# Second-level weight factors made by GpSimd instead of VectorE, with another order of some sums and reads

## The chip, the core and the metric

The kernel runs on one core of a Trainium2 chip. A core has five engines that work through their own instruction streams and wait for one another by semaphores: TensorE (PE in the profile; its weight loads are listed as PEld) multiplies matrices into PSUM banks, VectorE (DVE) and ScalarE (ACT) work on SBUF and PSUM, GpSimd (POOL) works on SBUF, and SyncE (SP) issues DMAs. The metric is the device time of one execution in microseconds; lower is better.

## The reference

64 batches of 256 tokens with 512 features, a 256 x 256 adjacency matrix of zeros and ones, four 512 x 512 weights and a bias. Two layers:

```python
h = relu(layernorm(x))
q, k, v = h @ Wq.T, h @ Wk.T, h @ Wv.T
rel = adj.T * (q @ k.T)
rel = rel / norm(rel, axis=2)
x = x + rel @ v
h = relu(layernorm(x))
x = x + (adj @ h) @ weight + bias
```

Everything is float32.

## The kernel before

The batches are worked on in 32 pairs. Since rel = h Wq.T Wk h.T, the kernel first makes one matrix M out of Wq and Wk (`m_sb`), and then, for each pair: g = h M (`project_g` or `g_by_two_levels`), v = h Wv.T (`project_v`, `v_by_two_levels`), the scores (`scores`), the update with v (`attend`, or `attend_and_v` in the steady state), the second norm (`ln1`), the product with the adjacency (`gather_steps`) and the product with `weight` (`mix_by_two_levels`).

The large products use Winograd's form of Strassen's scheme: each operand is cut in 2 x 2 blocks, and seven block products take the place of eight. Products 1, 2, 3 and 4 use blocks or one sum, 5, 6 and 7 use sums of blocks. The sums of the left operand are the four steps of `left_factors` (L166 to L178): step 0 makes the factor of product 7, step 1 (`total`) that of 5, step 2 that of 6, step 3 that of 3. The sums of the right operand are the four steps of `right_operands` (L128 to L140): step 0 makes the factor of 7, step 1 (`diff`) that of 5, step 2 that of 6, step 3 that of 4. Without a fourth room, `total` and `diff` are written over a block of the operand itself.

In a product, bank_a gathers products 1, 6, 7 and 4 one on top of the other, so each next product into it can start only when the sum so far has been read out, by a ScalarE copy for a first value and by a VectorE addition for later ones. bank_c gathers 5 and 3, and bank_b takes 2. `winograd_steps` gives the order; with `early` it is 1, 2, 5, 6, 3, 7, 4. `two_levels` (from pair 2 on) replaces products 2 and 3 by seven smaller products each, on 128 x 128 blocks. These small products are grouped as g1, g2, g3 and g4, and gathered in bank_e (`at_a`) and bank_d (`at_b`, `at_c`). Its parts a1, c5, a6, a7 and a4 are the first-level products, each followed by its read; `c` is a second read of bank_c for another block and has no product.

The second level needs sums of 128 x 128 blocks of the weights as well: `second_right` (L146) gives two sets of four `right_operands` steps for each of M (`m_second_steps`), Wv (`wv_second_steps`) and weight (`w_second_steps`), 24 instructions on VectorE. Step 1 of a set overwrites a block of the weight, which the first-level products 2 and 3 of pairs 0 and 1 still read.

The order of the work on TensorE, VectorE and ScalarE is the order in which the program is written: the code runs inside `manual_schedule(engines=in_order)`. `run_steps(steps, side)` issues each step of a product (its matmuls and its read) and then the instructions of `side` for that number, so that a side entry decides where in VectorE's and ScalarE's streams an instruction stands. GpSimd and SP take their work in the planner's order; GpSimd adds the bias to x (L723) and issues the output transfers (L794), SP the transfers that move 32 x 32 blocks for transposes (`place_blocks` L440, `place` L586) and most loads.

The stages that the change touches are `before_pairs` (M is made; VectorE's sums of Wq and Wk stand between the reads), `first_pairs` (pairs 0 to 3 started, the weights' second-level factors made), and `last_pairs` (the last three, a, b and c, where nothing follows that could fill the gaps). The transposition of a pair's h is eight VectorE instructions (`turned`, L450), after which the four sums of `new_ht` follow (`sums`, L173 to L176).

Of the kernel before, what the change touches and what calls it, by code (L numbers as in the profile page):

```python
# [9 lines left out]
F32 = mybir.dt.float32  # L10
# [3 lines left out]
ALU = mybir.AluOpType  # L14
# [5 lines left out]
def kernel(  # L20
# [38 lines left out]
    nc = tc.nc  # L59
    P = 128  # L60
    B, N, D = x.shape
    DC = D // P
    NC = N // P
# [5 lines left out]
    HT_ = T // 2  # L69
    HC = DC // 2  # L70
# [7 lines left out]
    work = ctx.enter_context(tc.tile_pool(name="work", bufs=1))  # L78
# [9 lines left out]
    def load(i, queue=nc.sync):  # L88
        X[i] = ring[i % len(ring)]
        queue.dma_start(out=X[i], in_=xs[i])  # L90
# [34 lines left out]

        return lambda j, k: w[:, j * HC : (j + 1) * HC, k * HD : (k + 1) * HD]

    def right_operands(b, t):  # L128

        sub = nc.vector.tensor_sub
        diff = t[3] if len(t) > 3 else b(0, 1)
        steps = [
            lambda: sub(t[1], b(1, 1), b(0, 1)),
            lambda: sub(diff, b(0, 1), b(0, 0)),
            lambda: sub(t[0], b(1, 1), diff),
            lambda: sub(t[2], b(1, 0), t[0]),
        ]
        return {1: b(0, 0), 2: b(1, 0), 3: b(1, 1), 4: t[2], 5: diff, 6: t[0], 7: t[1]}, steps  # L140
# [5 lines left out]
    def second_right(right, name):  # L146


        factors, steps = {}, []
        for n in (2, 3):  # L150
            t = const.tile([P, 3, P], F32, name=f"{name}_t{n}")
            factors[n], more = right_operands(
                lambda j, k, f=right[n]: f[:, j, ts(k, P)], [t[:, r] for r in range(3)]
            )
            steps += more
        return factors, steps

    def run(steps):
        for step in steps:
            step()  # L160

    def left_blocks(at):

        return lambda i, j: at[:, j * HC : (j + 1) * HC, i]

    def left_factors(a, s):  # L166

        v = nc.vector  # L170
        total = s[3] if len(s) > 3 else a(1, 0)
        steps = [
            lambda: v.tensor_sub(s[0], a(0, 0), a(1, 0)),  # L173
            lambda: v.tensor_add(total, a(1, 0), a(1, 1)),
            lambda: v.tensor_sub(s[1], total, a(0, 0)),
            lambda: v.tensor_sub(s[2], a(0, 1), s[1]),  # L176
        ]
# [642 lines left out]
    def before_pairs():  # L820
# [3 lines left out]
        pz = ps_m.tile([P, 512], F32, tag="pm", name="pz")  # L824
        for _ in range(8):
            nc.tensor.matmul(pz[:, :P], warm, warm, start=True, stop=True)
        m_left, left_steps = left_operands(
            work, wq_sb.rearrange("p c (h n) -> p c h n", h=NC), "ys", "m"
        )
        wk_t = work.tile([P, 4, HC, HD], F32, tag="hy", name="wk_t")  # L830
        m_factors, right_steps = right_operands(right_blocks(wk_sb), [wk_t[:, n] for n in range(4)])
# [1 line left out]
        stats, root, end, relus = ln0(0)  # L833
# [29 lines left out]
        def take(t, k, bank, first):  # L863
# [6 lines left out]

        look()
        transpose_adj()
        run([right_steps[1], left_steps[0], left_steps[1]])
        winograd(product_weights_moving(m_left, m_factors), take, {
            0: [load_wv],
            1: [left_steps[2], right_steps[2]],
            2: stats[0:2] + [lambda: load(1, nc.scalar)],
            3: [left_steps[3]] + stats[2:4] + [root, right_steps[0], lambda: load(2, nc.scalar)],
            4: [end] + relus + [right_steps[3]],
            5: m_steps[0:3] + [transpose_wv],  # L880
            6: m_steps[3:4],
# [48 lines left out]
    def first_pairs(exact):  # L930
# [26 lines left out]
            0: sums1[2:4] + masks[0:1], 1: masks[1:2] + squares[0:2] + stats[0:1],  # L957
            2: squares[2:4] + stats[1:2], 3: [norm_root] + stats[2:3],
            4: [inverse] + scales + [place] + stats[3:4] + [root], 5: [end] + w_steps[0:2],
            6: w_steps[2:4] + w_second_steps[0:4],  # L960
        })
        gs = g_operands(1)
        turned2, sums2 = transpose_blocks(2)
        project_v(1, {
            0: gs[0:2], 1: gs[2:3] + turned2[0:2], 2: gs[3:4] + turned2[2:4] + relus[0:2],
            3: turned2[4:6] + relus[2:4],
            4: turned2[6:8] + m_second_steps[0:4],
            5: m_second_steps[4:8] + turns[0:2], 6: turns[2:4],
        })
        place_blocks(3)  # L970
        masks, squares, norm_root, inverse, scales, place, turns = scores(1, {
            0: sums2[0:1], 1: sums2[1:2], 2: sums2[2:3], 3: sums2[3:4], 4: w_second_steps[4:8],
        })
        stats, *parts = ln1(0, exact)
        h_second = second_h.pop(2)()
# [4 lines left out]
        if exact:  # L980
            nc.vector.tensor_copy(adjt_r, adjt_sb)
        g, v = g_and_v(2, by_slot(layer_1(parts), {
            1: h_second + [inverse], 2: turned3[0:4], 3: scales + [place] + turned3[4:8],
            4: add_bias(0), 5: sums3[0:2],
        }))
        v_steps, rel_steps = attend_operands(1)
        y_products, y_steps = gather_steps(0, exact)
        run_steps(y_products, {
            0: wv_second_steps[0:4], 1: wv_second_steps[4:8], 2: y_steps[0:1], 3: v_steps[0:1],
        })  # L990
        y_second = second_of_y(0)
        totals, mean, row_squares, *norm0 = norm_by_scalar(flat(X[4]))
# [1 line left out]
        mixed = mix_and_v(0, g, v, {  # L994
            0: y_steps[2:4] + totals[0:2], 1: y_second[0:4] + totals[2:4],
            2: y_second[4:8] + [mean] + row_squares[0:2], 3: v_steps[1:2] + row_squares[2:4],
            4: turns + rel_steps[0:2] + norm0[0:2], 5: rel_steps[2:4] + v_steps[2:3] + sums3[2:4],
        })
        return norm0[2], v_steps[3:4], mixed, v

# [48 lines left out]
    def last_pairs(exact, relu0, v_last, mixed, v):  # L1049
# [37 lines left out]
        m = mix_by_two_levels(a)  # L1087
        root, end, relus, uppers, lowers = parts
        run_steps([
            m["a1"], m["c5"], lambda: run([m["a6"], m["c"]]), m["g1"], m["a7"], m["g2"], m["a4"],  # L1090
            m["g3"],
        ], {
            0: [root], 1: [inverse, end] + relus[0:2], 2: uppers[0:2],
            3: lowers[0:1] + relus[2:3], 4: lowers[1:2] + relus[3:4],
            5: uppers[2:4] + add_bias(b), 6: lowers[2:3], 7: lowers[3:4],
        })
        turn_at_once()
        m["g4"]()
# [8 lines left out]
        m = mix_by_two_levels(b)  # L1107
        root, end, relus, uppers, lowers = parts
        run_steps([
            m["a1"], m["c5"], lambda: run([m["a6"], m["c"]]), m["g1"], m["a7"], m["g2"], m["a4"],  # L1110
            m["g3"],
        ], {
            0: y_second[0:4] + [root], 1: y_second[4:8] + [end] + relus[0:2] + uppers[0:2],
            3: lowers[0:1] + relus[2:3], 4: lowers[1:2] + relus[3:4],
            5: uppers[2:4] + add_bias(c), 6: lowers[2:3], 7: lowers[3:4],
        })
        y_products, y_steps = gather_steps(c, exact)
        run_steps(y_products, {0: [m["g4"]], 2: y_steps[0:1]})
# [1 line left out]
        run(y_steps[1:2])  # L1120
        m = mix_by_two_levels(c)
        run_steps([
            m["a1"], m["c5"], m["g1"], lambda: run([m["a6"], m["c"]]), m["g2"], m["a7"], m["g3"],
            m["a4"], m["g4"],
        ], {0: y_steps[2:4] + y_second[0:4] + y_second[4:8]})

    first = dict(X), H[0]
    with tc.If(inexact < 1) as either:
# [33 lines left out]
```

## Time and profile before

| What | Value |
|---|---|
| median of 3 executions | 1709.56 us (1709.17 to 1711.31) |
| the profiled execution | 1708.38 us, its span 1706.3 us |
| TensorE busy | 1686.4 us (99%) |
| VectorE busy | 1479.2 us (87%) |
| ScalarE busy | 812.0 us (48%) |
| GpSimd busy | 213.0 us (12%) |
| first matmul starts, last one ends | 1.03 and 1700.14 us |

The span runs from the first to the last recorded instruction or transfer of the profiled execution; all times inside the kernel are counted from its start. In a timeline a row gives the start, the duration, the engine, the line, the operation, what it writes and reads, the shape, and how many instructions of that kind are merged in it. A bracket at the end gives how long the engine was idle before it, and what released it. In a row of TensorE, eight matmul records are one product of the first level.

### The profile page before, as it was taken

Reading aid. Unit: us, or ns where it says so; the run is one execution under the profiler, and the core shown is the slowest. Engines: PE = TensorE matmul, PEld = TensorE weight load, DVE = VectorE, ACT = ScalarE, POOL = GpSimd, SP = SyncE. Lnnn points to the kernel's source line nnn. Section 1 sums busy time; section 2 is a strip of 40 time slices with the busy share of each in tenths; the row PEclk is TensorE's granted clock in tenths of the full one; section 3 lists DMA queues with packets and bytes.
Section 4 is the critical chain, followed back from the end, with each engine's and each line's share of the span. In section 5 each row is a group of like instructions: output and inputs, shape, how many; then the busy total and the mean of one; then the engine's idle time right before and its main releaser. Section 6 shows DMA issues by size and latency. Waiting matters only on the chain.

```text
span 1706.3 us, 28450 instructions
## 1 busy us (share of the span) xinstructions
PE 1686.4 (99%) x10274; PEld 1530.5 (90%) x10274; DVE 1479.2 (87%) x3336; ACT 812.0 (48%) x1835; POOL 213.0 (12%) x167
## 2 busy tenths in 40 slices
PE   8999999999999999999999999999999999999998
PEld 7988999999999999999999999998999999999986
DVE  7888898888898888998888988888988889888777
ACT  4444545544445554445445455444455544453331
POOL 0011101111001111001111011110011110011111
PEclk9999999999999999999999999999999999999999
DMA  7414332234332343322343322433323433223101
GB/s 242 64 29 87 79 75 57 51 87 87 77 60 68 59 87 83 79 56 57 75 87 80 77 54 53 87 85 77 60 67 61 87 82 80 54 47 62 38 26 52
DMA packets 425734, 122.56 MB, mean 72 GB/s; under 512 B 398064, under 2 KB 398832, under 8 KB 425584
## 3 DMA queue, kind: packets, MB, share of 16 engines
q1 hardware_dynamic: 412992, 80.28, 25.5%
q0 software_dynamic: 8432, 32.51, 5.2%
q10 hardware_dynamic: 4160, 7.87, 1.3%
q8 instruction: 83, 1.36, 0.3%
q14 instruction: 67, 0.55, 0.1%
HBM read 38.27 MB, written 33.55 MB: 42 GB/s over the span
## 4 chain that ended last, share of the span: by engine, by line
PE 89%; DVE 5%; SPq 2%; ACT 1%; DMA 1%; issue 1%; DVEq 0%; ACTq 0%
PE bank_a L299 24%; PE bank_a L287 11%; PE bank_a L311 7%; PE bank_a L662 6%; PE bank_e L525 6%; PE bank_c L299 6%; PE py L739 6%; PE bank_d L525 5%; PE bank_c L311 3%; PE bank_c L287 3%; PE bank_c L662 3%; PE bank_e L478 3%; SPq L586 2%; PE bank_d L478 2%; PE bank_b L311 2%; PE bank_b L662 1%
## 5 line engine op out<-in xcount | busy, mean ns | idle before, releaser
L723 POOL TENSOR_TENSOR x_ring<-x_ring,bias_bc 128x512 f32<-128x512 f32 x128 | 188.2, 1491 | 745.1 <-DVE rel L559 437.1
L287 PE MATMUL bank_a<-ht,m_t 128*128 128x256 f32 x768 | 181.5, 379 | 0.6 <-DVE g L466 0.6
L299 PE MATMUL bank_a<-wv_t,ht 128*128 128x256 f32 x768 | 181.7, 379 | 0.0
L287 PEld LDWEIGHTS bank_a<-ht,m_t 128*128 128x128 f32 x768 | 145.8, 190 | 20.8 <-DVE g L466 1.0
L299 PEld LDWEIGHTS bank_a<-wv_t,ht 128*128 128x128 f32 x768 | 143.5, 190 | 18.3
L711 DVE TENSOR_TENSOR h<-h2c,h 128x512 fp32r<-128x512 f32 x128 | 86.5, 697 | 80.0 <-ACT h L707 80.0
L513 ACT COPY v<-bank_a 128x512 f32<-128x512 f32 x96 | 55.1, 574 | 207.9 <-PE bank_a L299 207.9
L364 ACT ACTIVATE blocks<-x_ring,sm 128x512 f32<-128x512 f32 x112 | 80.8, 722 | 125.1 <-DVE sm L361 123.3
L739 PE MATMUL py<-adjt_r,h 128*128 128x256 f32 x1024 | 126.8, 281 | 0.1
L342 ACT ACTIVATE h2c<-x_ring,nb,rs 128x512 f32<-128x512 f32 x128 | 97.5, 809 | 56.4 <-DVE nb L339 52.0
L299 PE MATMUL bank_a<-w_t,ys 128*128 128x256 f32 x512 | 121.4, 380 | 1.1 <-DVE x_ring L773 1.1
L739 PEld LDWEIGHTS py<-adjt_r,h 128*128 128x128 f32 x1024 | 120.8, 189 | 0.3 <-DVE h L711 0.3
L794 POOL DMA_DIRECT2D out_dram<-x_ring x31 | 24.0, 773 | 727.1 <-issue 525.8
L377 ACT ACTIVATE h<-x_ring,nb,rs 128x512 f32<-128x512 f32 x112 | 82.0, 802 | 65.9 <-PE bank_e L525 65.9
L299 PEld LDWEIGHTS bank_a<-w_t,ys 128*128 128x128 f32 x512 | 96.6, 190 | 15.1 <-DVE x_ring L773 1.9
L743 ACT COPY yt<-py 128x512 f32<-128x512 f32 x128 | 75.1, 587 | 71.5 <-PE py L739 44.7
L773 DVE TENSOR_TENSOR x_ring<-bank_a,x_ring 128x512 f32<-128x512 f32 x128 | 88.0, 687 | 22.4 <-PE bank_a L299 22.2
L311 PE MATMUL bank_a<-ht,gt 128*128 128x128 f32 x744 | 101.3, 279 | 0.4 <-DVE rel L559 0.4
L330 DVE BATCH_NORM_STATS2 st<-x_ring 128x6 f32<-128x512 f32 x144 | 97.9, 680 | 0.4
L557 ACT COPY rel<-bank_a 128x256 f32<-128x256 f32 x96 | 35.7, 372 | 130.4 <-PE bank_a L311 115.4
L311 PEld LDWEIGHTS bank_a<-ht,gt 128*128 128x128 f32 x744 | 90.4, 192 | 3.6 <-DVE rel L559 0.6
L450 DVE STREAM_TRANSPOSE ht<-blocks 128x256 f32<-128x256 f32 x248 | 87.6, 408 | 1.4 <-DMA blocks<-h 1.4
(221 smaller groups left out, 4006.4 us busy)
## 6 DMA issues: line engine op xcount, KB each, us to landing
blocks<-h SPq DMA_DIRECT2D x496, 64.0 KB, 2.3
out_dram<-x_ring POOLq DMA_DIRECT2D x31, 1024.0 KB, 4.8
x_ring<-in_x_dram SPq DMA_DIRECT2D x28, 1024.0 KB, 5.6
placed<-rel SPq DMA_DIRECT2D x496, 32.0 KB, 2.0
x_ring<-in_x_dram ACTq DMA_DIRECT2D x4, 1024.0 KB, 5.6
wq_sb<-in_L_gnn_Wq_dram SPq DMA_DIRECT2D x4, 256.0 KB, 5.0
wk_sb<-in_L_gnn_Wk_dram ACTq DMA_DIRECT2D x4, 256.0 KB, 6.0
wv_sb<-in_L_gnn_Wv_dram ACTq DMA_DIRECT2D x1, 1024.0 KB, 5.4
```

Source lines behind the costliest of these rows:

```text
L287: nc.tensor.matmul(bank[:, e * HT_ : (e + 1) * HT_], right[n][:, d, ts(e, P)], left[n][:, d, :], start=(start and e == 0 and d == 0), stop ...
L299: nc.tensor.matmul(bank[:, b * HD : (b + 1) * HD], left[n][:, d, ts(b, P)], right[n][:, d, :], start=(start and b == 0 and d == 0), stop=( ...
L311: nc.tensor.matmul(bank[:, ts(b, P)], right[n][:, d, ts(b, P)], left[n][:, d, ts(b, P)], start=(start and b == 0 and d == 0), stop=(d == H ...
L330: nc.vector.bn_stats(st[:, c, :], src[:, c, :])
L342: nc.scalar.activation(dst, src[:, c, :], AF.Relu, bias=nb[:, c : c + 1], scale=rs[:, c : c + 1])
L450: nc.vector.transpose(ht[:, d, half].rearrange("p (b n) -> p b n", b=NB), by_half[:, :, half, d])
L525: nc.tensor.matmul(out, left[k][n], right[k][n], start=start, stop=True, skip_group_check=True)
L662: nc.tensor.matmul(bank[:, ts(b, HD)], left[n][:, b], right[n][:, b], start=(start and b == 0), stop=True, skip_group_check=True,)
L711: nc.vector.tensor_sub(dst[:, 1, c, :], whole_h[c], dst[:, 0, c, :].bitcast(F32))
L723: (lambda c=c: add(xt[:, c, :], xt[:, c, :], bias_bc, ALU.add)) for c in range(TC)
L739: nc.tensor.matmul(pm[:, d, :], left[:, b * NC + m, ts(d0 + d, P)], right, start=(n == 0), stop=(n == len(terms) - 1),)
L773: nc.vector.tensor_add(xt[block], bank.rearrange("p (b e) -> p b e", b=NB), xt[block])
```

## The change

The 24 second-level steps of the weights are issued on GpSimd: `right_operands` gets the engine as a parameter, and `second_right` passes `nc.gpsimd`. They are no longer spread over the side entries but issued together: those of M and weight after `project_g(1)`, those of Wv after `place_blocks(3)`.

In `before_pairs`, Wq's `total` gets a room of its own (`m_room`), and the sums of Wq and Wk stand in another order among the reads and the statistics. In `first_pairs`, the sums of pair 2 and the transposes and sums of pair 3 stand at other side entries. In `last_pairs`, the second read of bank_c (`c`) follows product 7 instead of product 6, the differences `lowers` are issued two at a time and later, and the last pair's weight product takes its parts in the order of the other two, with the sums of y after its second product.

```diff
-    def right_operands(b, t):
-        sub = nc.vector.tensor_sub
+    def right_operands(b, t, engine=nc.vector):
         diff = t[3] if len(t) > 3 else b(0, 1)
+        def sub(out, x, y):
+            engine.tensor_tensor(out, x, y, ALU.subtract)
...
-                lambda j, k, f=right[n]: f[:, j, ts(k, P)], [t[:, r] for r in range(3)]
+                lambda j, k, f=right[n]: f[:, j, ts(k, P)], [t[:, r] for r in range(3)], nc.gpsimd
...
-        m_left, left_steps = left_operands(
-            work, wq_sb.rearrange("p c (h n) -> p c h n", h=NC), "ys", "m"
+        m_rooms = work.tile([P, 3, HC, HT_], F32, tag="ys", name="m_rooms")
+        m_room = work.tile([P, 4, 2, P], F32, tag="hs2", name="m_room")
+        m_room = m_room.rearrange("p a b n -> p (a b n)")[:, : HC * HT_]
+        m_left, left_steps = left_factors(
+            left_blocks(wq_sb.rearrange("p c (h n) -> p c h n", h=NC)),
+            [m_rooms[:, n] for n in range(3)] + [m_room.rearrange("p (c n) -> p c n", c=HC)],
...
-        run([right_steps[1], left_steps[0], left_steps[1]])
+        run([right_steps[1], left_steps[1]])
         winograd(product_weights_moving(m_left, m_factors), take, {
-            0: [load_wv],
-            1: [left_steps[2], right_steps[2]],
-            2: stats[0:2] + [lambda: load(1, nc.scalar)],
-            3: [left_steps[3]] + stats[2:4] + [root, right_steps[0], lambda: load(2, nc.scalar)],
+            0: [load_wv, left_steps[2], right_steps[2]],
+            1: [left_steps[3], left_steps[0]],
+            2: [right_steps[0]] + stats[0:1] + [lambda: load(1, nc.scalar)],
+            3: stats[1:4] + [root, lambda: load(2, nc.scalar)],
...
-            6: w_steps[2:4] + w_second_steps[0:4],
-        })
+            6: w_steps[2:4],
+        })
+        run(m_second_steps + w_second_steps)
...
-            4: turned2[6:8] + m_second_steps[0:4],
-            5: m_second_steps[4:8] + turns[0:2], 6: turns[2:4],
+            4: turned2[6:8], 5: turns[0:2], 6: turns[2:4] + sums2[0:1],
         })
         place_blocks(3)
+        run(wv_second_steps)
         masks, squares, norm_root, inverse, scales, place, turns = scores(1, {
-            0: sums2[0:1], 1: sums2[1:2], 2: sums2[2:3], 3: sums2[3:4], 4: w_second_steps[4:8],
+            0: sums2[1:2], 1: sums2[2:3], 2: sums2[3:4],
...
-            1: h_second + [inverse], 2: turned3[0:4], 3: scales + [place] + turned3[4:8],
-            4: add_bias(0), 5: sums3[0:2],
+            1: h_second + [inverse], 2: turned3[0:4], 3: scales + [place],
+            4: add_bias(0) + turned3[4:6], 5: turned3[6:8], 6: sums3[0:1],
...
-            0: wv_second_steps[0:4], 1: wv_second_steps[4:8], 2: y_steps[0:1], 3: v_steps[0:1],
+            0: sums3[1:3], 1: sums3[3:4], 2: y_steps[0:1], 3: v_steps[0:1],
...
-            4: turns + rel_steps[0:2] + norm0[0:2], 5: rel_steps[2:4] + v_steps[2:3] + sums3[2:4],
+            4: turns + rel_steps[0:2] + norm0[0:2], 5: rel_steps[2:4] + v_steps[2:3],
...
         run_steps([
-            m["a1"], m["c5"], lambda: run([m["a6"], m["c"]]), m["g1"], m["a7"], m["g2"], m["a4"],
+            m["a1"], m["c5"], m["a6"], m["g1"], lambda: run([m["a7"], m["c"]]), m["g2"], m["a4"],
             m["g3"],
         ], {
             0: [root], 1: [inverse, end] + relus[0:2], 2: uppers[0:2],
-            3: lowers[0:1] + relus[2:3], 4: lowers[1:2] + relus[3:4],
-            5: uppers[2:4] + add_bias(b), 6: lowers[2:3], 7: lowers[3:4],
+            4: lowers[0:2] + relus[2:4], 5: uppers[2:4] + add_bias(b), 7: lowers[2:4],
...
         run_steps([
-            m["a1"], m["c5"], m["g1"], lambda: run([m["a6"], m["c"]]), m["g2"], m["a7"], m["g3"],
-            m["a4"], m["g4"],
-        ], {0: y_steps[2:4] + y_second[0:4] + y_second[4:8]})
+            m["a1"], m["c5"], m["a6"], m["g1"], lambda: run([m["a7"], m["c"]]), m["g2"], m["a4"],
+            m["g3"], m["g4"],
+        ], {0: y_steps[2:4], 1: y_second})
```

The weight product of pair b changes as that of pair a does.

More of the change, by code (lines that the diff above doesn't have):

```diff
@@ L1109, in last_pairs @@
         run_steps([
-            m["a1"], m["c5"], lambda: run([m["a6"], m["c"]]), m["g1"], m["a7"], m["g2"], m["a4"],
+            m["a1"], m["c5"], m["a6"], m["g1"], lambda: run([m["a7"], m["c"]]), m["g2"], m["a4"],
             m["g3"],
@@ L1113, in last_pairs @@
             0: y_second[0:4] + [root], 1: y_second[4:8] + [end] + relus[0:2] + uppers[0:2],
-            3: lowers[0:1] + relus[2:3], 4: lowers[1:2] + relus[3:4],
-            5: uppers[2:4] + add_bias(c), 6: lowers[2:3], 7: lowers[3:4],
+            4: lowers[0:2] + relus[2:4], 5: uppers[2:4] + add_bias(c), 7: lowers[2:4],
         })
@@ L1122, in last_pairs @@
         run_steps([
-            m["a1"], m["c5"], m["g1"], lambda: run([m["a6"], m["c"]]), m["g2"], m["a7"], m["g3"],
-            m["a4"], m["g4"],
-        ], {0: y_steps[2:4] + y_second[0:4] + y_second[4:8]})
+            m["a1"], m["c5"], m["a6"], m["g1"], lambda: run([m["a7"], m["c"]]), m["g2"], m["a4"],
+            m["g3"], m["g4"],
+        ], {0: y_steps[2:4], 1: y_second})
     first = dict(X), H[0]
```

## The prediction

> **What bounds the kernel now.** I read the page's busy times first. TensorE (PE) works nearly all the time and VectorE (DVE) 87%; GpSimd (POOL) is almost idle.
>
> ```profile
> PE 1686.4 (99%) x10274; PEld 1530.5 (90%) x10274; DVE 1479.2 (87%) x3336; ACT 812.0 (48%) x1835; POOL 213.0 (12%) x167
> ```
>
> So only a wait of TensorE costs time. The waits, asked for the PE alone, name VectorE behind nearly all of them: results that VectorE reads out of a PSUM bank too late, or factors that it makes too late. The timeline puts them at the two ends of the run; between 140 and 1640 us the stalls are a few tenths each. Four places concern the change. First, the product of Wq and Wk:
>
> ```profile
> 13.48 0.69 DVE L137 TENSOR_TENSOR wk_t<-wk_sb,wk_t 128x512 f32<-128x512 f32 x1
> ...
> 14.31 1.97 PE L299 MATMUL bank_a<-wk_t,ys_m 128*128 128x256 f32 x8 [0.42 <-DVE wk_t L137]
> ...
> 16.50 1.97 PE L299 MATMUL bank_c<-wk_sb,ys_m 128*128 128x256 f32 x8 [0.22 <-DVE ys_m L176]
> ...
> 18.08 0.69 DVE L135 TENSOR_TENSOR wk_t<-wk_sb 128x512 f32<-128x512 f32 x1
> ```
>
> Three products in a row wait for a factor (the third, at 18.91, for the last row). A product of eight matmuls takes 1.73 us from start to start when nothing waits, so from the starts 12.00, 14.31, 16.50, 18.91 the true losses are 0.58, 0.46 and 0.68: 1.72 us. The brackets say less, because a matmul's end is modelled late. I use starts from here on.
>
> Second and third, in the first pairs, with the instructions that VectorE does ahead of the late read:
>
> ```profile
> 81.60 0.29 DVE L138 TENSOR_TENSOR m_t<-m_sb,m_t 128x128 f32<-128x128 f32 x1
> 82.00 1.43 DVE L589 STREAM_TRANSPOSE turned<-placed 128x256 f32<-128x256 f32 x4
> ...
> 86.77 1.16 PE L311 MATMUL bank_a<-ht,gt 128*128 128x128 f32 x8 [0.42 <-DVE rel L559]
> ...
> 103.64 2.72 DVE L450 STREAM_TRANSPOSE ht<-blocks 128x256 f32<-128x256 f32 x8
> ...
> 107.59 1.99 PE L287 MATMUL bank_a<-ht,m_t 128*128 128x256 f32 x8 [0.65 <-DVE g L466]
> ...
> 130.14 0.49 PE L525 MATMUL bank_e<-w_t,yt 128*128 128x128 f32 x2 [1.54 <-DVE x_ring L534]
> ...
> 132.00 0.69 DVE L175 TENSOR_TENSOR ht<-ht 128x512 f32<-128x512 f32 x1
> ...
> 132.71 0.69 DVE L176 TENSOR_TENSOR ht<-ht 128x512 f32<-128x512 f32 x1
> ...
> 134.06 1.13 PE L662 MATMUL bank_a<-placed,rel 128*128 128x256 f32 x4 [1.45 <-DVE x_ring L669]
> ```
>
> By starts these cost 0.59 (86.77), 0.80 (107.59), 1.70 (130.14) and 1.62 (134.06). Fourth, the last pairs' weight products, where the fourth product waits for the read of the one before:
>
> ```profile
> 1651.36 1.23 DVE L711 TENSOR_TENSOR h<-h2c,h 128x512 fp32r<-128x512 f32 x1
> ...
> 1653.25 1.99 PE L299 MATMUL bank_a<-w_t,yt 128*128 128x256 f32 x8 [0.45 <-DVE x_ring L773]
> ...
> 1678.49 1.17 DVE L711 TENSOR_TENSOR h<-h2c,h 128x512 fp32r<-128x512 f32 x1
> ```
>
> **What the Trainium skill says.** "SBUF — State Buffer", Who interferes with whom: a VectorE instruction with two SBUF inputs and a GpSimd instruction that reads SBUF lock each other out for a whole instruction. The trace agrees: the two L711 rows above took 1.23 and 1.17 us, each ending 0.55 us after a bias addition of GpSimd, and 0.68 elsewhere; a read that takes one input from PSUM kept its 0.69. "GPSIMD Engine Reference", Elementwise — side-by-side cycle accounting: a two-input add over 2048 elements takes 4497 ns. The trace has 1.28 us for 512 elements undisturbed (the first of the two at 1649.53). A line through both gives 2.1 ns an element and 0.2 us fixed: 0.47 us for 128 elements, an estimate. "Perfetto Trace Analysis", Tensor Engine Instruction: the end that the profile shows for a matmul is computed; hence starts.
>
> **Part 1, order of the Wq/Wk sums.** Same eight subtractions and additions; `total` gets a room of its own, so left_steps[1] need not follow left_steps[0]. VectorE's new order up to the product at 13.73 (12.00 + 1.73) is right 1, left 1, left 2, right 2. The last chunk of Wq lands at 8.88 and of Wk at 10.56, so right 2 ends about 11.3, ahead of bank_b's read at 12.27. Left 3 (12.88), left 0 (13.48), right 0 (14.08) follow at the 0.60 spacing of such rows, all before their products (15.46 and 17.19). TensorE could thus be 1.72 earlier. The four statistics now follow one another, and `root` stays at 18.00; without right 0 behind it, nb ends at 19.04 instead of 19.64. ScalarE then is the chain: relus 2.94, two copies of wvt, the copy of bank_a, four copies of ht, 6.5 us without the idle 0.83 it has today. The ht sum that the second product of project_g waits for ends at 26.28 and that product starts at 26.33 instead of 27.85. No moved step issues a DMA; the loads on ScalarE's queue keep their places behind the same copies, and SP's block transfers follow relus that come 1.5 earlier with the rest. Gain **1.5**.
>
> **Part 2, 24 second-level operations to GpSimd.** Each 128x128 row is 0.29 us on VectorE, 0.32 spaced: 7.8 us less there, of which 5.2 before 88 us. On GpSimd 24 x 0.47 = 11 us, where it does nothing before 99.12. The factors overwrite blocks that the whole first-level products read, so GpSimd starts m2 when TensorE has finished project_g(1)'s sixth product (67.2), w2 after w_steps, wv2 after project_v(1)'s sixth product (79.3): ready by about 71, 77 and 83, while the first user of m2 is at 99.8, of w2 at 119.3, of wv2 at 131.6. TensorE doesn't wait for them. POOL's queue holds only biases and output transfers behind them, the first at 99.12.
>
> The cost is the lock. Where w_steps and gs (eight two-input rows at 68.4 to 75.8) meet m2 and w2, the engines alternate. Each held row starts up to 0.47 later and runs 0.55: about 0.35 a row, six rows held, 2 us, against 1.3 us saved there (four w2 rows). bank_a's read in project_v(1) then ends about 0.4 later than its 78.28; TensorE needs it at 78.83, so nothing is lost. The unknown is the duration: 0.29 (the one-input GpSimd row on 128x128 at 1.20) to 1.28 (the 128x512 row). I take 0.47.
>
> After 80 us four m2 rows no longer fill the time in which the score blocks are in flight. The last of `placed` lands at 81.43, so the transposes start there, not at 82.00. To bank_a's read VectorE still does four transposes, four ht sums, two reads: 4.72 us as today, read done 86.22 against the 86.18 at which TensorE is free. Gain 0.59 - 0.09 = **0.5**.
>
> **Part 3, transposes and sums of pair 3.** Four of the eight transposes at 103.64 (1.33 us) leave the place ahead of bank_a's read, which ends 106.25 instead of 107.54, before TensorE is free at 106.79: 0.80 gained. They go behind lowers[2] and lowers[3]; with the sums moved into the gather in place of the eight wv2 rows, VectorE finishes yt's sum about 115.07 where TensorE, 0.8 earlier, wants it at 115.01: 0.1 back. Gain **0.7**. The stall at 130.14 stays: VectorE is idle 0.35 at 123.8, so it follows TensorE again, and its turns, rel sums and norm are as before. At 134.06 the two ht sums are gone: 2 starts 0.66 apart, 1.32 of the 1.62. Gain **1.3**.
>
> **Part 4, last pairs.** Pair a: the second read of bank_c and lowers[0] move behind the read of product 7, which ends 1652.58; the fourth product starts 1652.63, not 1653.25. But c and two lowers (0.6 each) now stand before g2's read, which ends 1654.71; g3 needs that bank at 1654.36 and starts 1654.76, not 1655.08. With the wait before g4 gone too, the gather starts 0.5 earlier; its fourth matmul of step 1 waits for lowers[3], which GpSimd's biases hold to about 1658.4: gain 0.45. Pair b: likewise g3 starts 1680.66 instead of 1680.46, and lowers[2:4], behind g3's reads and a bias that holds until 1683.15, end 1684.3 instead of 1684.12: loss 0.2. Pair c: all eight sums of y stand before a6's read, which ends 1694.0, so product 7 waits 1.3 us, in place of 1.56 us of stalls today; then g4 waits 0.45 for g3's read. The last read ends 1700.9 instead of 1700.75: loss 0.15. Together **+0.1**.
>
> Sum: 1.5 + 0.5 + 0.7 + 1.3 + 0.1 = 4.1 us. The profiled execution took 1708.38 (span 1706.3, 2.1 around it); it would be 1704.3. The median of three is 1709.56, 1.2 above the profiled one. I round to 4.0 for starts after waits: **1705.6**.
>
> **Rivals.** (1) VectorE held by GpSimd, ending slower. If a 128x128 GpSimd row takes as long as a 128x512 one (1.28), eight rows in project_v(1) come 8 x 1.2 - 1.3 - 0.55 = 7.7 us too late for bank_a's read, against 4.1 gained: 1713.2. It decides above (4.1 + 1.85)/8 + 0.1 = 0.84 us a row. For it: the 1.2 us L711 rows. Against: GpSimd's 128x128 row of 0.29. (2) The last pairs lose: lowers and y sums stand before reads at three places, and each may cost 0.7 more than I worked out if a bias falls badly: 1705.6 + 2 = 1707.6. For it: lowers already wait at 1678.49 today. (3) The prologue passes on only the 0.6 of nb (relus are then the chain), with half a microsecond held in part 2: 1707.0. (4) More: the stall at 130.14 shrinks, or the biases miss the lowers: 1704.3. (5) Nothing changes, the stalls being refilled by the next wait: 1709.5; against it, VectorE does 7.8 us less.
>
> **Numbers.** Main case 0.56 (1704.7 to 1706.5), rival 4 0.10, rivals 2 and 3 0.11 each, 5 0.05, 1 0.07. From 1704.0 to 1708.0 leaves out 5, 1 and the far edge of 4. About 0.2%, 3.4 us, is what a measurement tells from no change, so faster needs less than 1706.1: 0.47 of the main case, rival 4, and 0.14 of rivals 2 and 3, which lie around the edge; slower is rival 1; the rest is within.
>
> **What would show it.** No TensorE wait at 14 to 19, near 85 and 105 us; that of 130.14 still there at 1.5; that of 134.06 near 0.1; GpSimd rows of 128x128 near 0.47 from 65 to 83 us; new waits before g3 in the last pairs and before pair c's product 7. A GpSimd row over 0.8, or a wait before project_v(1)'s last product, proves me wrong; so does a start of the second project_g product later than 27.

## The result, and the profile after

| | before | changed | |
|---|---|---|---|
| median time | 1708.37 us (1707.29 to 1711.31, 17 runs) | 1705.60 us (1703.48 to 1707.79, 17 runs) | ratio 0.9981, 95% interval 0.9974 to 0.9989 |
| span of the profiled execution | 1706.26 us | 1701.41 us | 4.85 less |

The ratio says 3.2 us less, between 1.9 and 4.4; the medians differ by 2.8. The page's busy line after the change: TensorE's work is the same, VectorE has 24 instructions less, GpSimd 24 more.

```profile
PE 1684.2 (99%) x10274; PEld 1530.6 (90%) x10274; DVE 1472.9 (87%) x3312; ACT 811.3 (48%) x1835; POOL 226.7 (13%) x191
```

Line numbers from L138 to L826 are 3 higher than before, those further down 6 to 8, and the four steps of `right_operands` are now all L135. The timeline of the changed kernel, first at the product of Wq and Wk and the first two products of `project_g`:

```profile
13.71 1.89 PE L302 MATMUL bank_a<-wk_t,m_rooms 128*128 128x256 f32 x8
...
15.44 1.89 PE L302 MATMUL bank_c<-wk_sb,m_rooms 128*128 128x256 f32 x8
...
17.16 1.89 PE L302 MATMUL bank_a<-wk_t,m_rooms 128*128 128x256 f32 x8
...
23.52 1.93 POOL L135 TENSOR_TENSOR m_t<-m_sb 128x128 f32<-128x128 f32 x2 [22.02 <-ACT m_sb L874]
...
25.40 1.31 POOL L135 TENSOR_TENSOR wv_t<-wvt_sb 128x128 f32<-128x128 f32 x2
25.41 0.99 DVE L177 TENSOR_TENSOR ht<-ht 128x512 f32<-128x512 f32 x1 [0.28 <-ACT ht L434]
...
26.46 1.78 PE L290 MATMUL bank_c<-ht,m_sb 128*128 128x256 f32 x7 [0.44 <-DVE ht L177]
```

The three products stand 1.73 apart with no bracket: their waits are gone. The product at 26.46 is the one that started at 27.85. It still waits (0.60 by starts, 0.19 before): its sum L177 took 0.99 instead of 0.69, because GpSimd was reading beside it. These early GpSimd rows are steps 0 of M and Wv, which overwrite nothing, and which the planner put as early as their inputs allow. The rest of the second level, and what it does to VectorE:

```profile
65.97 0.46 POOL L135 TENSOR_TENSOR m_t<-m_sb 128x128 f32<-128x128 f32 x1
...
69.25 0.96 POOL L135 TENSOR_TENSOR w_sb<-w_sb 128x128 f32<-128x128 f32 x1 [2.29 <-DVE w_t L135]
...
69.81 0.94 DVE L135 TENSOR_TENSOR gt<-g 128x512 f32<-128x512 f32 x1
70.29 0.78 POOL L135 TENSOR_TENSOR w_t<-w_sb 128x128 f32<-128x128 f32 x1
...
79.80 1.42 DVE L592 STREAM_TRANSPOSE turned<-placed 128x256 f32<-128x256 f32 x4 [1.20 <-DMA placed<-rel]
```

A GpSimd row takes 0.45 to 0.46 when alone, and 0.78 to 0.96 where it meets the sums of g, which take 0.79 to 0.94 instead of 0.69. The score transposes now wait for their blocks to land, and no wait of TensorE is left at 85 us. Then the rest of the first pairs, and the last pairs:

```profile
104.70 1.89 PE L290 MATMUL bank_a<-ht,m_t 128*128 128x256 f32 x8
...
112.94 1.96 PE L302 MATMUL bank_c<-w_sb,yt 128*128 128x256 f32 x8
...
127.43 0.46 PE L528 MATMUL bank_e<-w_t,yt 128*128 128x128 f32 x2 [1.63 <-DVE x_ring L537]
...
129.93 1.13 PE L665 MATMUL bank_a<-placed,rel 128*128 128x256 f32 x4
...
1647.92 1.99 PE L302 MATMUL bank_a<-w_t,yt 128*128 128x256 f32 x8
...
1650.05 0.71 PE L528 MATMUL bank_e<-w_t,ys 128*128 128x128 f32 x4
...
1670.74 1.99 PE L302 MATMUL bank_a<-w_t,ys 128*128 128x256 f32 x8 [0.78 <-DVE x_ring L776]
...
1677.46 1.81 DVE L714 TENSOR_TENSOR h<-h2c,h 128x512 fp32r<-128x512 f32 x2
...
1689.20 1.99 PE L302 MATMUL bank_a<-w_t,ys 128*128 128x256 f32 x8 [1.14 <-DVE x_ring L776]
```

By starts the stalls are 0 (104.70), 0.25 (112.94), 1.79 (127.43), 0.22 (129.93), 0 (1647.92), 0.30 (1650.05), 0.94 (1670.74) and 1.30 (1689.20). What was 107.59, 130.14, 134.06 and 1653.25 is now 104.70, 127.43, 129.93 and 1647.92. The two differences of h at 1677.46 take 1.81 together; two of them take 1.28 where no bias addition runs.

For the experiments I cut every profiled execution at the same four instructions of TensorE and VectorE, counted from the span's start to its end. The first column ends at `project_g(0)`'s second product (27.85 before), the second at product 6 of the second attend (134.06), the third at the scores of pair b (1635.92), the fourth at VectorE's last read (1700.34), the last at the end of the span:

| us | start-up | first pairs | middle | last pairs | tail |
|---|---|---|---|---|---|
| before | 27.85 | 106.21 | 1501.86 | 64.42 | 5.92 |
| changed | 26.46 | 103.47 | 1501.21 | 64.70 | 5.57 |
| e_order | 26.79 | 106.53 | 1501.14 | 64.54 | 5.88 |
| e_gpsimd | 28.03 | 105.78 | 1503.08 | 64.43 | 5.94 |
| e_last | 27.78 | 106.53 | 1503.22 | 64.63 | 5.59 |
| e_vector | 26.65 | 107.94 | 1503.49 | 64.63 | 5.59 |
| e_pair3 | 28.06 | 105.76 | 1502.51 | 64.63 | 5.65 |
| e_long | 26.06 | 104.49 | 1503.99 | 64.61 | 5.60 |
| i_first | 26.58 | 101.93 | 1503.50 | 64.63 | 5.61 |
| i_last | 26.88 | 103.48 | 1501.96 | 64.35 | 5.60 |
| i_two | 26.57 | 101.95 | 1501.14 | 63.58 | 5.59 |
| i_three | 26.66 | 101.92 | 1503.60 | 62.76 | 5.61 |

The middle column is the same work in all twelve kernels (but for GpSimd's order in e_long and i_three), and differs by 2.9 us from one execution to another. The first column moves with the landing of Wq and Wk, and with TensorE's first microseconds: in e_pair3, for one, its matmuls are 0.43 apart instead of 0.22 until 12.85 us. So a single span can't tell these kernels apart. The columns of the first and the last pairs hold the places that the edits touch, but each comes from one execution, so I check them against the stalls.

### The profile page after: what moved, and what is told of

The parts are those of the page before. It is cut to its first block, busy times and chain, and to the rows that moved or that the text cites. A ratio compares the mean times of both kernels' runs of the same rounds, so it can differ in the third digit from the quotient of the medians.

```text
span 1701.4 us, 28459 instructions
## 1 busy us (share of the span) xinstructions
PE 1684.2 (99%) x10274; PEld 1530.6 (90%) x10274; DVE 1472.9 (87%) x3312; ACT 811.3 (48%) x1835; POOL 226.7 (13%) x191
## 4 chain that ended last, share of the span: by engine, by line
PE 91%; DVE 4%; SPq 2%; DMA 1%; ACT 1%; issue 1%; DVEq 0%; ACTq 0%
PE bank_a L302 24%; PE bank_a L290 12%; PE bank_a L314 7%; PE bank_c L302 6%; PE bank_e L528 6%; PE bank_a L665 6%; PE py L742 6%; PE bank_d L528 5%; PE bank_c L314 3%; PE bank_c L290 3%; PE bank_c L665 3%; PE bank_e L481 3%; SPq L589 2%; PE bank_d L481 2%; PE bank_b L314 2%; PE bank_b L665 1%
```

## Experiments: one part at a time

Each time below is a median beside runs of the kernel before on the same chip.

**Part 1 alone.** `before_pairs` as changed, all else as before (the diff is the one shown in the change).

> The kernel before with the new order of the sums of Wq and Wk alone (room of its own for total, sums ahead of the statistics). Theory: the three waits of TensorE between 14 and 19 us go, ScalarE then is the chain, and project_g's second product starts at 26.1 to 26.2 us: it started at 27.85 before and at 26.46 in the changed kernel, where one ht sum of VectorE took 0.99 instead of 0.69 beside GpSimd's first rows, which are not here. So 1.7 us less by the starts, and the stalls at 86.8, 107.6, 130.1 and 134.1 stay as before (0.6, 0.8, 1.7, 1.6). Rival: the gain of 1.7 needs nothing of the change but shows again as a longer stall behind it (scores or the first gather), and the whole is within 0.5 us of before.

Measured: 1708.43 us against 1709.89, ratio 0.9991 (0.9983 to 1.0000), which hardly tells it from before; the starts do:

```profile
11.21 1.56 PE L299 MATMUL bank_b<-wk_sb,wq_sb 128*128 128x256 f32 x6 [0.48 <-DMA wk_sb<-in_L_gnn_Wk_dram]
...
26.79 1.99 PE L287 MATMUL bank_c<-ht,m_sb 128*128 128x256 f32 x8
```

Counted from the product that waits for the last piece of Wk, so that the loads drop out, `project_g`'s second product comes 15.58 us later (26.79 - 11.21), against 17.25 before (27.85 - 10.60) and 15.88 in the changed kernel (26.46 - 10.58). The order gives 1.67, and GpSimd's early rows take 0.30 of it away again. The stalls behind stay (0.58, 0.80, 1.70, 1.62), and the first pairs are no shorter. They are in fact 0.3 longer: 0.34 is a stall in the scores of pair 0, where transposed blocks landed late; e_last, whose code there is that of before, has the same stall (its transposes start at 52.00, at 51.24 before). The rival falls: no stall that waits for a result of the sums refills the gain.

**Part 2 alone.** The engine changed, every side entry left where it was:

```diff
-                lambda j, k, f=right[n]: f[:, j, ts(k, P)], [t[:, r] for r in range(3)]
+                lambda j, k, f=right[n]: f[:, j, ts(k, P)], [t[:, r] for r in range(3)], nc.gpsimd
```

> The kernel before with the 24 second-level operations on GpSimd alone; every side entry otherwise as before. Theory: only the stall at scores(1) (0.59) goes, since four rows of 0.32 no longer stand ahead of its transposes; the early rows of GpSimd hold one ht sum and cost 0.2 to 0.3 at 28 us; the eight Wv rows leave VectorE's queue in the first gather, which had no stall, so the stalls of 0.8, 1.7 and 1.6 stay: 0.3 us less in all. Rival: the move of the 24 rows is what the whole gain comes from, 3 us less or more. Other rival: VectorE is held at every meeting, 1 us or more slower.

Measured: 1709.23 us against 1709.89, ratio 0.9996 (0.9988 to 1.0004). The stall of 0.59 at the scores of pair 1 is gone; those of 0.80, 1.79 and 1.55 are there. The first pairs are 0.43 shorter, with a stall of 0.29 in the scores of pair 0, where e_order and e_last have their 0.34. The expected loss of 0.2 to 0.3 at 28 us did not come: the second product of `project_g` waits 0.23, 0.19 before. The move of the 24 instructions is worth the stall of 0.59 by itself, in the first pairs; the time of the whole can't be told from that of before, and a gain of 3 us is excluded. The larger gains in the first pairs come from what is done with the freed places.

**The other side of part 2.** The changed kernel, with the 24 operations on VectorE again (the argument `nc.gpsimd` taken away).

> The changed kernel with the 24 operations on VectorE again, at the same places of the program. Theory: sixteen rows of 0.32 (5.1 us) stand on VectorE between the sums of weight and of g, less 0.6 us in which GpSimd held it, with 0.65 us of idle time to take it: the reads in project_v(1) come 3 to 4 us late and its last product waits for them, and the eight Wv rows (2.6 us) ahead of the scores' reads cost up to 1.5 more: 3.5 to 5.5 us slower than the changed kernel, that is no faster than before or slower. Rival: VectorE has room for these rows, and the gain of the change is one of order alone: within 0.7 us of the changed kernel.

Measured: 1709.82 us against 1709.89, ratio 1.0001 (0.9993 to 1.0010); the changed kernel stands at 0.9981. With these 24 operations issued together, the order of the change needs GpSimd. The place is the expected one, the last product of `project_v(1)`, but the price has two halves. The timeline of this run, and its busy times by window (the window and its length, then the busy time and count of PE, PEld, DVE, ACT and POOL, the granted TensorE clock, the DMA share and GB/s):

```profile
79.98 0.66 DVE L518 TENSOR_TENSOR v<-bank_a,v 128x512 f32<-128x512 f32 x1
...
80.69 3.58 PE L302 MATMUL bank_a<-wv_t,ht 128*128 128x256 f32 x8 [2.62 <-DVE v L518]
```

```profile
77.50:80.60 3.10, 0.57 (x3) 0.16 (x1) 3.10 (x9) 0.00 (x0) 0.00 (x0) 0.99 0.26 42
80.60:84.20 3.60, 3.51 (x9) 2.87 (x10) 3.57 (x11) 0.00 (x0) 0.00 (x0) 0.54 0.33 43
```

TensorE waits 2.8 us by starts for the read at 79.98. Then the eight matmuls take 3.58 us instead of 1.89, at a granted clock of 0.54: the next product starts at 84.10 instead of 79.64, so a wait of 2.8 us costs 4.5. The Trainium skill, "TensorE: Matmul & The Clock Gate", What's actually happening, states that the array falls to half its rate after at least one idle window of about 3.4 us. Half the rate agrees with the 0.54, but here 2.8 us of waiting was enough. At the scores no stall came up, so the expected 1.5 there did not exist: TensorE was already late by more than VectorE was. The waits at the two places of pair 3 are gone here too (none at the first, 0.29 at the second), so those gains do not seem to need GpSimd, though TensorE runs 4.5 us later here. No run left the 24 operations on VectorE at their old places and moved the rest.

**Part 3 taken away.** The changed kernel with the transposes and sums of pair 3 as before:

```diff
-            1: h_second + [inverse], 2: turned3[0:4], 3: scales + [place],
-            4: add_bias(0) + turned3[4:6], 5: turned3[6:8], 6: sums3[0:1],
+            1: h_second + [inverse], 2: turned3[0:4], 3: scales + [place] + turned3[4:8],
+            4: add_bias(0), 5: sums3[0:2],
...
-            0: sums3[1:3], 1: sums3[3:4], 2: y_steps[0:1], 3: v_steps[0:1],
+            2: y_steps[0:1], 3: v_steps[0:1],
...
-            4: turns + rel_steps[0:2] + norm0[0:2], 5: rel_steps[2:4] + v_steps[2:3],
+            4: turns + rel_steps[0:2] + norm0[0:2], 5: rel_steps[2:4] + v_steps[2:3] + sums3[2:4],
```

> The changed kernel with the transposes and sums of pair 3 at their places of before. Theory: the stall of 0.8 at 107 us comes back and that of 0.2 at 130 us grows to 1.5 to 1.6, since two ht sums of 0.66 stand ahead of its read again; the 0.25 at 113 goes: 1.9 us slower than the changed kernel (1.8 to 2.2 by TensorE's start after 130 us). Rival: VectorE, freed of the Wv rows there, makes up for it, and only one of the two stalls comes back: 0.8 or less.

Measured: 1708.50 us against 1710.37, ratio 0.9991 (0.9983 to 1.0000), 0.0010 above the changed kernel's, which is 1.7 us; the two intervals overlap, so the starts have to decide. The first pairs are 2.29 longer than in the changed kernel; 0.28 of it is a stall at the scores of pair 1, where blocks landed late, so 2.0 belongs to the edit. Both stalls are back, 0.80 at 107.48 and 1.55 at 133.82:

```profile
131.76 0.68 DVE L178 TENSOR_TENSOR ht<-ht 128x512 f32<-128x512 f32 x1
...
133.09 0.68 DVE L672 TENSOR_TENSOR x_ring<-bank_a,x_ring 128x512 f32<-128x512 f32 x1
133.82 0.73 PEld L665 LDWEIGHTS bank_a<-placed,rel 128*128 128x128 f32 x4 [1.58 <-DVE x_ring L672]
```

The sums of h stand ahead of the read that the product at 133.82 waits for. This is the largest part of the change.

**Part 4 alone.** `last_pairs` as changed, all else as before.

> The kernel before with the new order in the last three pairs alone. Theory, from the two profiles: pair a gives 0.4, the rest takes 0.7, so the last read of a bank comes 0.2 to 0.4 us later counted from TensorE's start of the last pairs, and the time is the same within 0.5 us. The prediction's own sum was 0.1 us of gain. Rival: the time between the last read and the end (1.5 us shorter in the profile of the changed kernel, with one less wait on the output's queue) belongs to this order, and the kernel is 1 us faster.

Measured: 1709.28 us against 1709.89, ratio 0.9994 (0.9986 to 1.0002). The table answers better: the last pairs take 64.42 to 64.54 in the three kernels with the old order (before, e_order, e_gpsimd) and 64.61 to 64.70 in the six with the new order as it stands, 0.2 longer. The tail, from the start of the last read to the end, is 5.88 to 5.94 with the old order and 5.57 to 5.65 with the new, 0.3 shorter. In the old order SyncE issues two output transfers 0.46 us apart at the very end, in the new one the last comes 0.64 after the one before it (first the kernel before, then e_last):

```profile
1700.45 0.37 SPq L777 DMA_DIRECT2D out_dram<-x_ring  x1
1700.91 0.42 SPq L792 DMA_DIRECT2D out_dram<-x_ring  x1
```

```profile
1701.98 0.34 SPq L787 DMA_DIRECT2D out_dram<-x_ring  x1
1702.62 0.34 SPq L792 DMA_DIRECT2D out_dram<-x_ring  x1
```

Both theories hold a part: a loss to the last read, and a tail that makes up for it. That the spacing of the transfers is what shortens the tail I argue from these rows; no run changed it alone.

## Experiments: the lock between GpSimd and VectorE

**More and longer GpSimd rows.** GpSimd follows the program's order, and a useless addition follows each second-level operation:

```diff
+    def longer():
+        nc.gpsimd.tensor_tensor(long_room, bias_bc[:, :256], bias_bc[:, 256:], ALU.add)
...
-            steps += more
+            steps += [(lambda s=s: (s(), longer())) for s in more]
...
-    in_order = {EngineType.PE, EngineType.DVE, EngineType.Activation}
+    in_order = {EngineType.PE, EngineType.DVE, EngineType.Activation, EngineType.Pool}
```

> The changed kernel with GpSimd in the order of the program, and each of the 24 second-level operations followed by one more GpSimd addition on 128x256 that nothing needs. This keeps GpSimd busy from 62 to about 93 us, in rows of 0.45 and 0.7 to 0.8. Theory: VectorE's rows with two SBUF inputs each wait for about one such row; eight of them ahead of the reads in project_v(1) make 4 to 5 us against 0.65 of idle time, and the sums of pair 2 some more: TensorE waits 3 to 6 us at 76 to 88 us, and the kernel is no faster than before. Rival: the lock costs little because the engines alternate without loss, and the kernel stays within 1 us of the changed one.

Measured: 1706.84 us against 1710.37, ratio 0.9981 (0.9973 to 0.9989), the same as the changed kernel, though its first pairs are 1.0 us longer. My theory here was wrong in size. VectorE's sums of weight and g are held one after another, as it said:

```profile
67.92 0.83 DVE L135 TENSOR_TENSOR w_sb<-w_sb 128x512 f32<-128x512 f32 x1
68.16 1.17 POOL L150 TENSOR_TENSOR long_room<-bias_bc 128x256 f32<-128x256 f32 x1
68.78 1.10 DVE L135 TENSOR_TENSOR w_t<-w_sb 128x512 f32<-128x512 f32 x1
69.29 0.90 POOL L135 TENSOR_TENSOR m_t<-m_sb 128x128 f32<-128x128 f32 x1
```

But a row behind a 0.45 one takes 0.83 and one behind a 0.73 one takes 1.10 to 1.24, instead of 0.69: they lose 0.14 and 0.41 to 0.55. A row of VectorE does not pay for the whole GpSimd row, because that row is already running when it starts. The row at 68.78, for one, finds 0.55 left of the GpSimd row that ends at 69.33, and loses 0.41.

This holds in all twelve traces. I take every VectorE `tensor_tensor` with both inputs in SBUF that starts at least 0.15 us after the start of a GpSimd one, and at least 0.2 us before its end: 447 rows. Each loses the time that is left, less 0.13 to 0.14 us. So it ends 0.54 to 0.56 us after the GpSimd row if it is 512 wide, beside GpSimd rows of all three lengths; 0.28 to 0.29 if 256, and 0.15 if 128 (both beside rows of 512 only). GpSimd's rows wait likewise: those of 0.45 and 0.73 take 0.90 and 1.17 in this stretch, and the engines alternate.

The eight sums start 1.0 us apart instead of 0.7, and TensorE waits 0.69 at 78.00, not 3 to 6. The start-up shows the other half of the edit: the ht sum is not held, and the second product waits 0.30 instead of 0.60.

**Where the lock does cost.** In the last two weight products, the second four sums of y placed behind the read of product 6:

```diff
-            0: y_second[0:4] + [root], 1: y_second[4:8] + [end] + relus[0:2] + uppers[0:2],
+            0: y_second[0:4] + [root], 1: [end] + relus[0:2] + uppers[0:2], 2: y_second[4:8],
...
-        ], {0: y_steps[2:4], 1: y_second})
+        ], {0: y_steps[2:4], 1: y_second[0:4], 2: y_second[4:8]})
```

> The changed kernel, and in the last two weight products the second four sums of y behind the read of product 6. Theory: product 7 of pair b no longer waits 0.94 and that of pair c no longer 1.3, of which 0.2 to 0.6 comes back at the reads behind them: 1.5 to 2.0 us less to the last read. Rival: the second-level products behind them wait for the same sums, or the differences of h come no earlier and the gather of pair c waits for them: 0.5 us or less.

Measured: 1706.03 us against 1710.37, ratio 0.9978 (0.9968 to 0.9988); the last pairs are only 0.35 shorter. In the last pair the wait before product 7 falls from 1.30 to 0.25 as expected. In pair b its 0.94 goes, and 1.59 comes at the second-level products behind it:

```profile
1671.17 2.69 POOL L726 TENSOR_TENSOR x_ring<-x_ring,bias_bc 128x512 f32<-128x512 f32 x2 [14.69 <-DVE ys L178]
1671.37 1.37 DVE L178 TENSOR_TENSOR ys<-ys 128x128 f32<-128x128 f32 x1
...
1672.78 1.24 DVE L179 TENSOR_TENSOR ys<-ys,ys 128x128 f32<-128x128 f32 x1
...
1674.40 0.71 PE L528 MATMUL bank_e<-w_t,ys 128*128 128x128 f32 x4 [1.43 <-DVE x_ring L537]
```

Two sums of 0.28 to 0.29 us take 1.37 and 1.24. The norm, moved ahead of them, had started the relu that the bias additions wait for. The relu ends at 1671.09; the bracket names a sum that ended at 1671.12, but the same row in i_three names the relu. Each bias row of 1.3 to 1.4 us holds one sum for 0.9 to 1.1. So the rival came, in effect and in size, but for a cause that I had not written down: a step put later ran into an engine that the step put before it had set going. It is the lock of the prediction's rival 1, at the price of a 128x512 row, in a place where the changed kernel's sums meet no such row.

## Experiments: what was left to take

The stall of 1.79 at 127.43 was still there, as predicted. Two transposes go one step ahead, the norm's root ahead of two sums of rel, its reciprocal behind the read, and the fourth sum of rel, which was behind it already, to the next stage:

```diff
-            2: y_second[4:8] + [mean] + row_squares[0:2], 3: v_steps[1:2] + row_squares[2:4],
-            4: turns + rel_steps[0:2] + norm0[0:2], 5: rel_steps[2:4] + v_steps[2:3],
+            2: y_second[4:8] + [mean] + row_squares[0:2],
+            3: v_steps[1:2] + row_squares[2:4] + turns[0:2],
+            4: turns[2:4] + norm0[0:1] + rel_steps[0:2],
+            5: rel_steps[2:3] + norm0[1:2] + v_steps[2:3],
...
-        return norm0[2], v_steps[3:4], mixed, v
+        return norm0[2], rel_steps[3:4] + v_steps[3:4], mixed, v
```

> The changed kernel, and in the first weight product two of the four transposes of the scores one step earlier, the norm's reciprocal and the third sum of rel after the reads of the fourth product. Theory: the stall of 1.8 at 127.4 us was VectorE's queue (transposes, two sums and a norm that waits 0.5 for ScalarE) ahead of that read, so it falls to 0.2 to 0.4, and 0.2 to 0.3 of it comes back at 130: TensorE is 1.2 to 1.6 us earlier after 130. Rival: the next wait refills it (the attend's products need the same sums), and less than 0.5 is left.

Measured: 1705.21 us against 1710.37, ratio 0.9970 (0.9957 to 0.9982). The stall is 0.41, the 0.22 behind it is gone, and 0.26 comes up at 137.56: the first pairs are 1.54 shorter than in the changed kernel, 1.28 with that last stall. The theory holds by the starts; the interval of the ratio overlaps with that of the changed kernel. Several rows were moved together, so which of them mattered most stays open.

Then this edit, with the new place of the sums of y in the last pair alone.

> The changed kernel with the edit of i_first, and with the second four sums of y behind the read of product 6 in the last pair alone, where no bias addition of GpSimd can meet them. Theory: 1.3 us from the first pairs as there, and 1.05 of the 1.3 at product 7 of the last pair: 2.3 us less than the changed kernel, 0.9966 to 0.9970 of before. Rival: pair b was where i_last gained and the last pair gives nothing: no better than i_first.

Measured: 1702.20 us against 1710.52, ratio 0.9955 (0.9942 to 0.9969). First pairs 1.52 and last pairs 1.12 shorter than in the changed kernel, as the theory has it. For pair b, GpSimd then makes the four sums before its bias additions (`late` is a new parameter of `left_factors` that `second_of_y` passes on, VectorE elsewhere):

```diff
-            lambda: v.tensor_sub(s[1], total, a(0, 0)),
-            lambda: v.tensor_sub(s[2], a(0, 1), s[1]),
+            lambda: late.tensor_tensor(s[1], total, a(0, 0), ALU.subtract),
+            lambda: late.tensor_tensor(s[2], a(0, 1), s[1], ALU.subtract),
...
-        y_second = second_of_y(b, "hs2")
+        y_second = second_of_y(b, "hs2", nc.gpsimd)
...
-    in_order = {EngineType.PE, EngineType.DVE, EngineType.Activation}
+    in_order = {EngineType.PE, EngineType.DVE, EngineType.Activation, EngineType.Pool}
```

> As i_two, with GpSimd in the order of the program, and the second four sums of y of pair b made by GpSimd ahead of its bias additions. Theory: GpSimd's early rows no longer hold the ht sum at 26 us (0.3 us), product 7 of pair b no longer waits 0.94 since its read has only the norm's two short rows ahead of it, and the sums are there 0.5 us before the second-level products ask for them: 1.2 us less than i_two, less what the gather of pair c then waits longer for the differences of h (up to 0.6). Rival: the four rows come too late (each 0.53, behind VectorE's first four), or hold VectorE's first four, and the 0.94 shows again at the second-level products: 0.3 less or nothing.

Measured: 1702.46 us against 1710.52, ratio 0.9949 (0.9936 to 0.9963). The last pairs are 62.76, 0.82 less than i_two:

```profile
1670.16 0.46 POOL L179 TENSOR_TENSOR ys<-ys,ys 128x128 f32<-128x128 f32 x1
...
1670.88 1.99 PE L302 MATMUL bank_a<-w_t,ys 128*128 128x256 f32 x8
1670.93 0.42 DVE L537 TENSOR_TENSOR x_ring<-bank_e,x_ring 128x256 f32<-128x256 f32 x1
1671.24 2.51 POOL L726 TENSOR_TENSOR x_ring<-x_ring,bias_bc 128x512 f32<-128x512 f32 x2 [0.62 <-ACT h2c L345]
```

GpSimd's last sum ends at 1670.62, 0.6 before the bias takes the engine, and the product at 1670.88 starts without a wait. Of the 1.2 us expected, 0.82 shows there and 0.3 at the second product of `project_g`, which waits 0.30 instead of 0.61. The times of i_two and i_three can't be told apart, but both are below the changed kernel's: the upper ends of their intervals, 0.9969 and 0.9963, lie under its lower end of 0.9974.

## Why the prediction was right

**Its total.** 4.0 us were predicted, 3.2 (1.9 to 4.4) measured. TensorE is 4.13 us ahead after the first pairs (129.93 against 134.06), where the steps add up to 4.0. The rest of the 4.85 us between the two profiled spans is 0.65 in the middle, which no edit touches, and the last pairs and tail, which nearly cancel. That the predicted time itself, 1705.6, was met to the tenth is luck in part: it was counted from 1709.56, the median of three runs, and more runs of the same kernel put that at 1708.37.

**Part 1, predicted 1.5: measured 1.39.** The three waits are gone and ScalarE's copies became the chain, as said: alone, the order gives 1.67. The step that failed is in part 2, "GpSimd starts m2 when TensorE has finished project_g(1)'s sixth product". That holds only for the three steps that hang on the block of product 2, which start at 65.44. Those of product 3's block start at 62.05, after the fourth product. The planner put the steps that only read far ahead, at 23.5 us, and one held the sum that this part's gain hung on, for 0.30. Without that hold the product would have started 0.17 earlier than predicted, so two misses nearly cancel here.

**Part 2, predicted 0.5: measured 0.59.** The GpSimd row was put at 0.47 and took 0.45 to 0.46. The factors were ready at 67, 74 and 79 us, earlier than 71, 77 and 83, since part of the steps needed no waiting and TensorE was 1.4 us ahead. The prediction's own figures, 81.43 and 4.72, put the read at 86.15 and not at 86.22, and so give the whole 0.59. The lock was put at "about 0.35 a row, six rows held, 2 us"; four sums of g lost 0.10 to 0.25 each, 0.6 together. The Trainium skill's "SBUF — State Buffer", Who interferes with whom, gave the right question, whether the two engines meet, and its rule of an exclusive lock fits the 447 rows above: who starts second waits for the end of the other's instruction. What the prediction had wrong is how much of that instruction is left: it put a whole row of 0.47 of GpSimd's ahead of each, and the four sums found 0.24 to 0.40 left; its 0.55 for the rest of a held row is what the rows show. The prediction's "0.68 elsewhere" for L711 is not so either: two more rows beside a bias took 0.82 and 1.31 (1655.89 and 1681.27), as the same rule has it.

**Part 3, predicted 0.7 and 1.3: measured 0.55 and 1.40.** The stall at 107.59 gave its 0.80; at the sum of yt 0.25 came back instead of 0.1. The stall at 130.14 stayed (1.79). e_pair3 gives 2.0 for both, against 2.0 predicted.

**Part 4, predicted +0.1: nothing that can be told from zero.** The waits before g3 (0.30 against 0.4), before the last pair's product 7 (1.30 against 1.3) and before its g4 (0.39 against 0.45) are where they were put. The sum to the last read is a loss of 0.2 to 0.3 and not a gain: of the 0.5 that pair a's product gave to the gather of pair b, put at 0.45 in the end, 0.23 was left at that gather's end; pair b lost 0.15 (0.2 predicted) and pair c 0.35 (0.15 predicted). The term missing from the sum was the tail, 0.3 shorter.

**The rivals.** 1 needs rows over 0.84 us and did not come; its own price, nearly a whole row lost for every row held, was too high for alternating rows, as e_long shows (0.14 for rows of 0.45, 0.41 for most of 0.73). 2 fell: e_last lost nothing in time. 3 fell: e_order passed on 1.67, not 0.6. 5 fell: the stalls were not refilled. 4 did not happen by itself, but i_first shows that its stall could be had.

## What to carry to other kernels

Work off a busy engine is worth little by itself (0.6 us here); it is worth what can then be moved out of the queue ahead of a late read (2.0 us for pair 3). The gain at the product of Wq and Wk needed no freed engine at all, only another order. Before moving a step later in a queue, ask what the steps left ahead of it set going on the other engines, and whether it will meet that. When an engine takes its work in a planner's order, steps that only read may run far earlier than where they are written, and what they meet there belongs into the sum.

## What the runs showed of the hardware that was not expected

- A TensorE wait of 2.8 us was paid for 1.6 times: the eight matmuls behind it took 3.58 us instead of 1.89 at a clock of 0.54 (e_vector). No wait of up to 1.8 us inside the pairs did that. The length of one wait does not decide it alone: in the start-up of i_last and i_three the matmuls fell back to 0.43 us apart after two waits of 1.0 to 1.6 us with about 1 us of work between, while e_order went through one of 2.1 us there at full rate. In e_vector, i_last and i_three the record has the clock at half for 3.41 us, and then whole again.
- A VectorE row with two SBUF inputs loses what is left of the GpSimd row that it meets, less 0.13 to 0.14 us, whatever its own length: up to 0.31 beside rows of 0.45, 0.56 beside rows of 0.73 and 1.1 beside rows of 1.3.
- The 1500 us in the middle, the same in all kernels here, differed by 2.9 us between twelve executions, nearly as much as this change is worth.
